# A Mamba scan whose states are turned by fp32 products with the identity instead of TensorE's transpose mode

## The chip, the cores and the metric

The kernel runs on one core of a Trainium2 chip. TensorE (PE) multiplies, VectorE (DVE), ScalarE (ACT) and GpSimd (POOL) work elementwise, and DMA queues move data. Each engine takes its instructions in the order in which the program lists them and waits on semaphores for the others. The metric is the device time of one execution in microseconds, as the median of several runs; lower is better.

## What is computed

A network of four layers on an image batch `x` of 2 x 256 x 32 x 32, all in fp32: two Mamba blocks, a convolution attention, linear attention with a mixture of experts, softmax attention with a second mixture of experts. Only the Mamba blocks matter here. With d = 512 inner channels, n = 16 states and L = 1024 tokens per image, a block computes

```python
dA = jnp.exp(delta[..., None] * A)
dBu = delta[..., None] * Bm[:, :, None, :] * xs[..., None]
def step(hst, ins):
    dA_t, dBu_t, C_t = ins
    hst = dA_t * hst + dBu_t
    y_t = jnp.einsum('bdn,bn->bd', hst, C_t)
    return (hst, y_t)
_, ys = jax.lax.scan(step, h0, (...))
y = jnp.swapaxes(ys, 0, 1) + xs * Dp
y = y * jax.nn.silu(res)
out = y @ out_w + out_b
```

Each block has input projections, a causal convolution of four taps and a softplus ahead of this, and a layer norm behind it.

## The kernel before

Both images together are 2048 tokens, taken as four chunks of 512 tokens per block, so eight chunks in all (`units`). Channels lie on the 128 partitions, four groups of them (`NDC`), tokens along the free dimension.

`Mamba.front` prepares a chunk: projections (L323), the convolution as products with diagonal matrices (L351), softplus and `du` (L396 to L431; the elementwise part of it on POOL at L425 to L431). `Mamba.scan` is the chunk's main loop over the 16 states. For each state n:

- a DMA broadcasts the row of B over the partitions (L477), and POOL makes `du * B` in two halves of 128 x 1024 (L481), into `h` tiles. Six such tiles exist, so three states' worth.
- for each of the four channel groups, ACT makes the decay `exp(delta * A)` into one of three PSUM tiles `da` (L490), and DVE runs the recurrence along the tokens in place, a scan of 512 steps (L494).
- `rest` sums over the states with the weight C. C is a number per token and h has tokens along the free dimension, so h is turned: for each 128 tokens, TensorE turns four 128 x 128 blocks into a PSUM tile `ht` of 128 tokens x 512 channels (L460; three such tiles), and DVE adds C times it to `ya` (L469). For states 0 and 10 ACT makes the product instead (L467).

`rest` is a generator: the turns of a state and their reads are issued one step at a time between the scans of the next states, through `before`. Between them `paced` also issues steps of the next chunk's `front`, of the last chunk's `back` and of the weights for the convolution behind the Mamba blocks (`taps.make`). In the eighth chunk there is no next front; 112 steps of that convolution (`early`, L818) are issued there instead.

`Mamba.back` finishes a chunk: gates (L517), then per channel group one PSUM sum of the skip term (L540) and of the two partial sums `ya` and `yb`, turned back by plain products with the identity (L545), the gating (L549), the output projection (L557, L561), the layer norm and its transposes (L192, in a helper).

The order in the source is not the order of the program: a scheduler with a cost for every instruction decides, engine by engine, what is listed ahead of what, within the dependencies and the numbers of buffers. The program carries the order that it chose.

A turn and the product that turns `ya` back are written differently. `nc.tensor.transpose(out, in, ident)` is a matmul instruction in transpose mode; L545 is `nc.tensor.matmul(out, lhsT=in, rhs=ident)`, whose result is `in` transposed times the identity.

Of the kernel before, what the change touches and what calls it, by code (L numbers as in the profile page):

```python
# [19 lines left out]
P = 128  # L20
# [226 lines left out]
class Mamba:  # L247
# [187 lines left out]
    def scan(self, j, before, between, start=False):  # L435

        net, nc, m, scanp = self.net, self.net.nc, self.m, self.scanp
        xs, bd, ct, delta, du = self.chunks[j]
        state, first = self.state, self.first(j)
        ya = self.two.tile([P, TPC, DI], F32, tag="ya", name=f"{m}_ya_{j}")
        yb = self.one.tile([P, TPC, DI], F32, tag="yb", name=f"{m}_yb_{j}")
        self.chunks[j] = xs, ya, yb
        G = 2
        half = [P, G, TC]

        def keep(n, hs):  # L450
            for g, h in enumerate(hs):
                nc.scalar.copy(state[:, n, g * G : (g + 1) * G], h[:, :, TC - 1])

        def rest(n, hs):


            for i in range(TPC):
                ps = self.ps_ht.tile([P, DI], F32, tag="ht", name=f"{m}_ht_{j}_{n}_{i}")
                for dc in range(NDC):
                    nc.tensor.transpose(  # L460
                        ps[:, dc * P : (dc + 1) * P], hs[dc // G][:, dc % G, i * P : (i + 1) * P],
                        net.ident,
                    )
                yield
                c = ct[:, i, n : n + 1]
                if n in (0, self.ASIDE):
                    nc.scalar.activation((yb if n else ya)[:, i, :], ps, AF.Copy, scale=c)  # L467
                else:
                    nc.vector.scalar_tensor_tensor(  # L469
                        ya[:, i, :], ps, c, ya[:, i, :], ALU.mult, ALU.add  # L470
                    )
                if i == 0 and first:
                    keep(n, hs)

        for n in range(NS):
            b = scanp.tile([P, TC], F32, tag="b", name=f"{m}_b_{j}_{n}", bufs=4)
            nc.sync.dma_start(b, bd[n].partition_broadcast(P))  # L477
            hs = []
            for g in range(NDC // G):
                h = scanp.tile(half, F32, tag="h", name=f"{m}_h_{j}_{n}_{g}", bufs=6)  # L480
                made = (nc.vector if start and n == 0 else nc.gpsimd).tensor_mul(  # L481
                    h, du[:, g * G : (g + 1) * G, :], b.unsqueeze(1).to_broadcast(half)
                )
                hs.append(h)
            self.product = made
            for dc in range(NDC):
                da = self.ps_da.tile([P, TC], F32, tag="da", name=f"{m}_da_{j}_{n}_{dc}")
                i = dc * NS + n
                with net.tc.issue_after(net.loaded.ins):
                    net.decayed = nc.scalar.activation(  # L490
                        da, delta[:, dc, :], AF.Exp, scale=self.aneg[:, i : i + 1]
                    )
                h = hs[dc // G][:, dc % G, :]
                nc.vector.tensor_tensor_scan(  # L494
                    h, da, h, 0.0 if first else state[:, n, dc : dc + 1], ALU.mult, ALU.add
                )


                next(before, None)
                if n or dc:  # L500
                    next(between, None)
            before = chain(before, rest(n, hs))
        for _ in between:
            pass
        return before
# [1295 lines left out]
```

## Time and profile before

| | |
|---|---|
| median of 3 runs | 2160.94 us (2155.56 to 2163.15) |
| the profiled execution | 2164.79 us as timed, span 2163.1 us |
| mean granted TensorE clock | 0.909 of full speed |
| PE, busy | 1894.6 us (88%), 9652 instructions |
| PE weight loads (PEld), busy | 1343.4 us (62%), 9652 instructions |
| DVE, busy | 1403.5 us (65%), 2173 instructions |
| ACT, busy | 891.1 us (41%), 1589 instructions |
| POOL, busy | 1027.9 us (48%), 726 instructions |

The profile is taken by the hardware in one execution. A matmul shows as two records, a load of the stationary operand (PEld) and the multiplication (PE). Matmuls overlap, and their ends are modelled, so PE's busy time is not its work. The span in 40 slices of 54 us, in tenths of busy time:

```profile
PE   6889799897988888799999999949999699859996
...
DVE  6999989999999998897414575652222534432223
...
PEclk9869888898979999799999999959999799979997
```

The Mamba blocks are the first 19 slices or so (scans run from 49.6 to 1054.1 us), and there DVE is nearly always busy. PEclk is the clock that TensorE was granted. What follows, up to the end of the span, is the rest of the network; the change doesn't touch it. Other views used below give one line of code's instructions with their durations, what each engine waited for, TensorE's instructions in order of time, and busy times in chosen stretches.

### The profile page before, as it was taken

How to read it: one execution, taken by the hardware profiler on the slowest of the kernel's cores; microseconds unless marked ns; L12 is line 12 of the kernel's file. 1: busy time of each engine (PE TensorE's matmuls, PEld its weight loads, DVE VectorE, ACT ScalarE, POOL GpSimd, SP SyncE). 2: the span in 40 equal slices, each digit the busy share in tenths (PEclk: the TensorE clock that was granted, in tenths of full speed). 3: DMA queues.
4: the chain of work that ended last, by engine and by line, in shares of the span. 5: the costliest groups of instructions: out<-in, count | busy, mean ns of one | idle time of the engine just before them, and what ended most of it. 6: DMA issues, size and time to landing. Idle time of an engine off the chain costs nothing.

```text
span 2163.1 us, 27234 instructions
## 1 busy us (share of the span) xinstructions
PE 1894.6 (88%) x9652; PEld 1343.4 (62%) x9652; DVE 1403.5 (65%) x2173; ACT 891.1 (41%) x1589; POOL 1027.9 (48%) x726
## 2 busy tenths in 40 slices
PE   6889799897988888799999999949999699859996
PEld 2465566555565545455655556639998467659994
DVE  6999989999999998897414575652222534432223
ACT  4677666676777667553213433311110222201111
POOL 3787887959688785964316410013332000023331
PEclk9869888898979999799999999959999799979997
DMA  3121121112112111310030100038998200069997
GB/s 108 45 69 40 42 66 40 54 35 63 45 47 61 40 49 31 82 43 25 10 55 1 49 15 10 20 116 301 329 329 306 83 10 10 20 216 328 333 331 285
DMA packets 90497, 223.85 MB, mean 103 GB/s; under 512 B 35467, under 2 KB 51728, under 8 KB 79732
## 3 DMA queue, kind: packets, MB, share of 16 engines
q1 hardware_dynamic: 77636, 198.29, 27.4%
q0 software_dynamic: 7728, 19.15, 3.0%
q10 hardware_dynamic: 4992, 4.59, 0.7%
q8 instruction: 80, 1.31, 0.3%
q14 instruction: 61, 0.50, 0.1%
HBM read 204.60 MB, written 19.37 MB: 104 GB/s over the span
## 4 chain that ended last, share of the span: by engine, by line
PE 27%; issue 14%; POOL 8%; DVE 8%; DMA 4%; ACT 1%; POOLq 0%; ACTq 0%; DVEq 0%; SPq 0%
PE acc L818 4%; POOL x L1578 3%; POOL l_yd L1628 3%; PE av L1332 3%; PE h L1155 3%; PE early_acc L818 2%; PE sc L1306 2%; DMA l_yd<-y,target 2%; DVE m_h L494 2%; PE w L1164 1%; DVE m_ya L469 1%; DMA x<-l_zd,source 1%; PE m_ht L460 1%; PE mm_t L192 1%; POOL m_h L481 1%
## 5 line engine op out<-in xcount | busy, mean ns | idle before, releaser
L481 POOL TENSOR_TENSOR m_h<-m_du,m_b 128x1024 f32<-128x1024 f32 x254 | 594.4, 2363 | 222.5 <-PE m_ht L460 124.0
L460 PEld LDWEIGHTS m_ht<-ident,m_h 128*128 128x128 f32 x2048 | 265.5, 155 | 300.7 <-issue 110.7
L460 PE MATMUL m_ht<-ident,m_h 128*128 128x128 f32 x2048 | 357.6, 304 | 98.1 <-DVE m_ya L469 71.9
L490 ACT ACTIVATE m_da<-m_delta,m_aneg 128x512 f32<-128x512 f32 x512 | 349.2, 691 | 210.5 <-DVE m_h L494 206.3
L1578 POOL DMA_INDIRECT x<-l_zd,source x82 | 84.6, 1032 | 576.1 <-DVE source L1523 218.6
L469 DVE SCALAR_TENSOR_TENSOR m_ya<-m_ht,m_ct,m_ya 128x512 f32<-128x512 f32 x448 | 319.3, 731 | 30.7 <-PE m_ht L460 30.4
L494 DVE TENSOR_TENSOR_SCAN m_h<-m_da,m_state,m_h 128x512 f32<-128x512 f32 x256 | 317.9, 1268 | 23.3 <-POOL m_h L481 14.5
L494 DVE TENSOR_TENSOR_SCAN m_h<-m_da,m_h 128x512 f32<-128x512 f32 x256 | 303.4, 1208 | 21.1 <-ACT m_da L490 13.5
L1608 PEld LDWEIGHTS h<-xts,we 128*128 128x128 f32 x2528 | 298.3, 194 | 6.1 <-issue 2.2
L1608 PE MATMUL h<-xts,we 128*128 128x128 f32 x2528 | 299.1, 277 | 1.6 <-issue 1.5
L1615 DVE TENSOR_TENSOR hid<-hid,h 128x512 f32<-128x512 f32 x79 | 54.3, 687 | 266.8 <-PE h L1608 266.8
L1614 ACT ACTIVATE hid<-h 128x512 f32<-128x512 f32 x79 | 47.2, 597 | 411.3 <-PE h L1608 411.3
L1622 PE MATMUL o<-we,hid 128*128 128x256 f32 x632 | 150.6, 380 | 3.9 <-DVE hid L1615 2.3
L1628 POOL DMA_INDIRECT l_yd<-y,target x79 | 79.0, 1000 | 136.4 <-DVE y L1627 131.6
L1622 PEld LDWEIGHTS o<-we,hid 128*128 128x128 f32 x632 | 113.7, 190 | 17.8 <-DVE hid L1615 3.0
L351 PE MATMUL m_conv<-m_pre,m_taps 128*128 128x512 f32 x240 | 114.3, 596 | 1.6 <-ACT m_gate L521 1.6
L818 PE MATMUL early_acc<-x,early 128*98 128x448 f32 (+24 forms) x308 | 98.6, 447 | 0.0
L818 PE MATMUL acc<-x,pair 128*98 128x416 f32 (+21 forms) x308 | 93.8, 453 | 0.0
L1627 DVE COPY y<-o 128x256 f32<-128x256 f32 x79 | 33.5, 425 | 70.0 <-PE o L1622 69.7
L323 PE MATMUL m_in<-x,m_in_sb 128*128 128x512 f32 x128 | 70.4, 665 | 9.2 <-ACT m_pre L327 5.4
L517 PE MATMUL m_g<-x,m_gate_sb 128*128 128x512 f32 x128 | 69.6, 650 | 7.3 <-ACT m_gate L521 4.7
L818 PEld LDWEIGHTS acc<-x,pair 128*98 128x98 f32 x308 | 48.0, 168 | 40.6 <-issue 35.4
(313 smaller groups left out, 2797.7 us busy)
## 6 DMA issues: line engine op xcount, KB each, us to landing
we<-in_l_experts_dram SPq DMA_DIRECT2D x82, 1536.0 KB, 9.4
m_b<-m_bd SPq DMA_DIRECT2D x128, 256.0 KB, 3.3
w<-in_l_w_dram SPq DMA_DIRECT2D x21, 256.0 KB, 4.1
l_zd<-l_z SPq DMA_DIRECT2D x7, 512.0 KB, 2.8
l_yl<-l_yd SPq DMA_DIRECT2D x10, 256.0 KB, 5.9
l_yl<-l_yd ACTq DMA_DIRECT2D x10, 256.0 KB, 6.5
early<-taps SPq DMA_DIRECT2D x7, 343.0 KB, 4.9
pair<-taps SPq DMA_DIRECT2D x7, 343.0 KB, 6.0
```

The source lines that it names most:

```text
L323: nc.tensor.matmul(ps, lhsT=self.in_sb[:, kc, mc * P : (mc + 1) * P], rhs=self.xt[:, kc, tok], start=(kc == 0), stop=(kc == NCC - 1),)
L351: nc.tensor.matmul(ps, lhsT=self.taps[:, dc * 4 + k, :], rhs=pre[:, dc, k : k + TC], start=(k == 0), stop=(k == 3),)
L460: nc.tensor.transpose(ps[:, dc * P : (dc + 1) * P], hs[dc // G][:, dc % G, i * P : (i + 1) * P], net.ident,)
L469: nc.vector.scalar_tensor_tensor(ya[:, i, :], ps, c, ya[:, i, :], ALU.mult, ALU.add)
L481: made = (nc.vector if start and n == 0 else nc.gpsimd).tensor_mul(h, du[:, g * G : (g + 1) * G, :], b.unsqueeze(1).to_broadcast(half))
L490: net.decayed = nc.scalar.activation(da, delta[:, dc, :], AF.Exp, scale=self.aneg[:, i : i + 1])
L494: nc.vector.tensor_tensor_scan(h, da, h, 0.0 if first else state[:, n, dc : dc + 1], ALU.mult, ALU.add)
L818: nc.tensor.matmul(a[:, lo - 16 * k : hi - 16 * k, co : co + n], lhsT=lhsT, rhs=self.x[:, kc, b, lo - r0 : hi - r0, ci : ci + n], start=(u ...
L1578: nc.gpsimd.indirect_dma_start(out=x, out_offset=None, in_=zd[:, :], in_offset=bass.IndirectOffsetOnAxis(ap=source[:, g : g + 1], axis=0), ...
L1608: nc.tensor.matmul(ps[:, at], lhsT=w12[:, s, kc, at], rhs=xt[:, kc * P : (kc + 1) * P], start=(kc == 0), stop=(kc == NCC - 1),)
L1622: nc.tensor.matmul(ps[:, :C], lhsT=ht[:, mc * P : (mc + 1) * P], rhs=w[:, 8 + mc, :], start=(mc == 0), stop=(mc == NHC - 1),)
L1628: nc.gpsimd.indirect_dma_start(out=yd[g], out_offset=bass.IndirectOffsetOnAxis(ap=target[:, g : g + 1], axis=0), in_=y, in_offset=None, bo ...
```

## The change

In `rest`, the four transposes of a turn become four matmuls with the same operands, without transpose mode: `lhsT` is the block of h, `rhs` the identity, and each is a sum of its own (`start` and `stop` both set).

```diff
                 for dc in range(NDC):
-                    nc.tensor.transpose(
-                        ps[:, dc * P : (dc + 1) * P], hs[dc // G][:, dc % G, i * P : (i + 1) * P],
-                        net.ident,
+                    nc.tensor.matmul(
+                        ps[:, dc * P : (dc + 1) * P],
+                        lhsT=hs[dc // G][:, dc % G, i * P : (i + 1) * P], rhs=net.ident,
+                        start=True, stop=True,
                     )
                 yield
                 c = ct[:, i, n : n + 1]
```

Nothing else in the source changes. The instructions are the same in number on every engine, apart from one table load of ACT, but the scheduler lists many of them in another order. The changed file is one line longer, so everything behind L463 moves down by one line.

## The prediction

> **What bounds the kernel now.** I read the list of costly groups first, then each line's own view, then the waits, the tables by stretch and the timelines.
>
> The edit is on L460, so the first question is what its successor costs. The kernel already has that instruction: L545 multiplies 128x128 fp32 blocks by the same identity, without transpose mode. Its lines:
>
> ```profile
> L460 PE MATMUL m_ht<-ident,m_h x2048: 270/273/478, 51.2 to 1059.3; 128*128 128x128 f32 x187
> L460 PEld LDWEIGHTS m_ht<-ident,m_h x2048: 137/141/356, 50.9 to 1059.1; 128*128 128x128 f32 x187
> ...
> L545 PE MATMUL m_y<-ident,m_ya x256: 272/275/421, 201.7 to 1068.1; 128*128 128x128 f32 x128
> L545 PEld LDWEIGHTS m_y<-ident,m_ya x256: 190/192/337, 201.3 to 1068.0; 128*128 128x128 f32 x128
> ```
>
> The durations (min/median/max in ns) look alike; the counts don't. The loops issue 8 chunks x 16 states x 4 x 4 = 2048 turns, and the trace has 2048 records: one each. L545 issues 8 x 4 x 4 = 128 products on ya, and the trace has 256 records: two each. The other fp32 products agree (L561: 8 x 4 x 4 = 128 in the code, 256 records). So one fp32 product is two loads and two passes in this trace, one turn is one of each.
>
> What a record costs is the pitch, not the duration, since records overlap. From TensorE's timeline:
>
> ```profile
> 449.92 0.60 PE L460 MATMUL m_ht<-ident,m_h 128*128 128x128 f32 x4
> 450.36 1.02 PE L540 MATMUL m_y<-m_xs,m_skip 128*128 128x512 f32 x2
> 451.22 1.05 PE L545 MATMUL m_y<-ident,m_ya 128*128 128x128 f32 x8
> ```
>
> Four turns take 450.36 - 449.92 = 0.44 us: 0.110 each (0.109 over long runs). The two 512-column records take 0.86, 0.43 each. Eight L545 records last 1.05 us of which the last is 0.275: (1.05 - 0.275)/7 = 0.111, so a product is 2 x 0.112 = 0.224 us.
>
> Now who sets the end of the Mamba stage (49.6 to 1054.1 us, eight chunks of 115 to 143 us):
>
> ```profile
> 658.20:778.80 120.60, 103.94 (x507) 66.76 (x505) 117.42 (x135) 84.61 (x129) 96.87 (x53) 0.92 0.16 40
> ...
> 910.90:1054.10 143.20, 136.06 (x606) 81.01 (x605) 117.93 (x132) 64.58 (x92) 84.08 (x41) 1.00 0.13 35
> ```
>
> Columns: stretch, length, busy time of PE, its loads, DVE, ACT, POOL, then the clock. In the sixth chunk DVE is busy 117.4 of 120.6 us; the other middle chunks are alike. In the eighth PE takes over: 136 of 143, because the early convolution (L818) runs there. But "busy PE" counts overlapping ends twice over, so I count its work by records times pitch. For the second quarter of the fourth chunk, 438.1 to 470.6 us (16 scans):
>
> ```profile
> L460 PE MATMUL m_ht<-ident,m_h 128*128 128x128 f32 x68 | 9.8, 276 | 0.9 <-DVE m_ya L469 0.9
> L351 PE MATMUL m_conv<-m_pre,m_taps 128*128 128x512 f32 x20 | 9.4, 593 | 0.0
> L370 PE MATMUL m_xd_ps<-m_xs,m_xp_sb 128*48 128x512 f32 x8 | 3.8, 602 | 0.2 <-ACT m_xs L363 0.2
> L545 PE MATMUL m_y<-ident,m_yb 128*128 128x128 f32 x24 | 3.2, 275 | 0.0
> L545 PE MATMUL m_y<-ident,m_ya 128*128 128x128 f32 x24 | 3.2, 275 | 0.0
> L540 PE MATMUL m_y<-m_xs,m_skip 128*128 128x512 f32 x6 | 3.1, 594 | 0.0
> ```
>
> With three more 512-wide records (L399, L517) that is 68 x 0.109 + 48 x 0.112 + 37 x 0.43 = 28.7 us of work in 32.5. There is little room.
>
> **The change, part by part.** *Passes.* 2048 x (0.224 - 0.109) = 236 us more of TensorE time, some 29 per chunk. Nothing else is added; DVE's reads (L469), POOL's products (L481) and the transfers stay in number.
>
> How much of the 29 is hidden? I repeat the count above (width/512 x 0.43 for other widths) for each quarter of each chunk, add 0.115 per turn, and take what exceeds the quarter's length. In the quarter shown: 28.7 + 7.8 = 36.5, so 4.0 over (4 from unrounded counts). Chunk by chunk: second 5.3, third 4.1, fourth 6.5, fifth 7.3, sixth 5.6, seventh 0: sum 28.8 us. The fourth quarters have 10 us to spare each, the first chunk 25, so neither gives anything. The cover is DVE's own work; where it is gone (front matmuls of the next chunk, the projections of the last one), a slot goes at PE's pace. Bounds: whole chunks instead of quarters have room for all of it (PE's work afterwards is 110 to 122 us against lengths of 119 to 132), so 0; stretches of 3.4 us instead of quarters give 73. The ring of three PSUM buffers and six h tiles spans about 2 to 3 states, 16 to 24 us, so I stay with the quarter: 29.
>
> *Eighth chunk.* PE's work there is 130.6 us in 143.2. With 248 turns at 0.115 (28.5) it is 159.1: at least 15.9 over if all idle time is used, 28.5 if none. The idle part lies mostly before 967 us, where the convolution is thin, so I take the middle, 22.
>
> *Loads.* The first load of a group that finds PE waiting is longer by 192 - 141 = 51 ns. It is on the path only where DVE waits for a turn, 28 times: 1.4 us. The second load runs beside the first pass (L545 keeps 0.112 with it).
>
> *Order.* The scheduler writes another order: the reads of turned states now trail the scans by 7 scans on average in the middle chunks (5.5 before, counted from the built order), and each chunk has a run of seven to nine scans without a read. An h tile is free for POOL only when its state is turned, and the turn needs a PSUM buffer that a read has freed. Between the read of state 1 and the first scan of state 4, DVE's work shrinks from 9 to 12 us to 2.2 to 3.4. In it must fit four groups' last turn and one POOL product of 2.36 us (L481). At one prompt turn of 4 x 0.224 + 0.27 = 1.2, that is 3.6 us: short by 0.2 to 1.4 in each of seven chunks, some 5 us. If the last turn comes 4 us after the read that frees its buffer, as it does at these places before (3.9 to 4.4 us in the timelines), 4 x 7 = 28 more. POOL's 16 elementwise products of the next front (1.27 us each, L425 to L431) also stand closer together, within three states: 16 x 1.27 + 2 x 4.73 + 2.36 = 32 against some 29 of DVE. That is 3 us a chunk, but where PE already stretches the quarter it overlaps. I take 12 for the order, ends 0 and 33. What waits behind a late read on DVE's queue is the next scan, and for that ACT's decays (L490, three PSUM buffers).
>
> A gain is possible too. Today DVE waits in the chunks before the eighth:
>
> ```profile
> DVE m_ya L469 <- PE m_ht L460: 19.7, 21, 2.3
> DVE m_h L494 <- ACT m_da L490: 17.4, 15, 2.6
> DVE m_h L494 <- POOL m_h L481: 12.0, 9, 3.2
> ```
>
> 49 us in all; a deeper lag could swallow some. I count none, since turns get slower.
>
> *Clock.* All pitches are at full clock; these chunks run at 0.74 to 0.92. The stretches that fell to half are thin ones:
>
> ```profile
> 111.82 2.49 PE L460 MATMUL m_ht<-ident,m_h 128*128 128x128 f32 x10
> ...
> 111.80:115.20 3.40, 3.17 (x14) 2.11 (x12) 3.40 (x4) 3.12 (x5) 2.61 (x2) 0.51 0.13 39
> 115.20:118.60 3.40, 1.65 (x10) 0.98 (x9) 3.40 (x5) 3.31 (x4) 3.15 (x2) 1.00 0.05 17
> 118.60:122.00 3.40, 2.45 (x8) 1.37 (x8) 3.40 (x5) 2.03 (x4) 3.40 (x2) 0.50 0.18 60
> ```
>
> After 10 short records in 3.4 us (115.2 to 118.6) the clock halves; the fuller stretch before it, which the timeline shows as almost nothing but turns, ended in a rise to 1.00. Eight products in 3.4 us are 16 records, half the time: I expect the clock near 1.00 and use the full-speed pitch.
>
> The Trainium skill, "TensorE: Matmul & The Clock Gate", section "Terms", says that transpose mode is four times faster for fp32: the rule against this change. The trace's two records against one make it 2.05. By four the extra would be 2048 x 0.327 = 670 us, and the eighth chunk alone would grow by about 69. The same page's Part 4 says that transposes do not lift the clock; the rise at 115.2 after turns alone disagrees.
>
> *Sum:* 22 + 29 + 12 + 1 = 64 us on the profiled execution's span of 2163.1 (2164.8 as timed), giving 2229. That execution lies 3.9 above the median of the runs, 2160.9, so I forecast 2225.
>
> **The rivals.** (A) *All on the path*: turns and their readers go in lockstep, nothing is hidden: 2161 + 236 = 2397. For it: PE waits for DVE's reads (71.9 us) and DVE for PE. Against: fourth quarters are half empty on PE. (B) *Hidden*: the new order spreads the passes evenly and the eighth chunk fills its idle time with little left over: within 6 us of 2161. Against: 15.9 over in the eighth even then. (C) *Faster*: the deeper lag ends DVE's 49 us of waits above, the eighth chunk pays its 16: 2161 - 49 + 16 = 2128. It decides if PE keeps below DVE in every stretch, so that no read finds its turn missing; the quarters of the second to sixth chunk speak against it. (D) *One pass*: a product by the identity stays one record at 0.112; then 2048 x 0.003 = 6 us of PE and only the order's 5 to 33: about 2175. All 256 products of L545 having two records is against it.
>
> **How the numbers follow.** Mine 0.80, A 0.05, B 0.05, C 0.04, D 0.06. The forecast's own ends: 16 in the eighth chunk alone, 2177; 28.5 + 73 + 33 + 1 = 135, 2296. A few us inside these ends, 2178 to 2292, leaves A, B, C and most of D outside, some 2 in 10. A measurement of this kernel tells 0.3% (6.5 us) from no change. Faster: C, 0.04. Same: B and a little of D, 0.07. Slower: the rest, 0.89.
>
> **What would show it.** 4096 records on the turn's line at a pitch of 0.112; the eighth chunk 16 to 28 us longer with PE over 95% busy; second and third quarters longer by 4 us or more; DVE's waits for turns well above 30.4 us; clock near 1.00 from 160 to 1050 us; nothing moved after the Mamba stage. I am wrong if the records stay 2048, or if a chunk's length follows DVE alone.

## The result and the profile after

| | median | runs | ratio to before |
|---|---|---|---|
| before | 2159.39 us | 2155.56 to 2163.15 (4, with one run more than in the table above) | |
| after | 2325.65 us | 2322.88 to 2328.68 (4) | 1.077 [1.0745, 1.0795] |

The change makes the kernel 166 us slower, where 64 were forecast and 2292 us was the upper end. The profiled execution after has a span of 2321.2 us, 158.1 more than before. The Mamba stage, from the first scan to the last, grew by 152.9 us (1004.4 to 1157.3), so the loss is there.

The costly groups of the page after, then the turn's own line (min/median/max in ns):

```profile
L482 POOL TENSOR_TENSOR m_h<-m_du,m_b 128x1024 f32<-128x1024 f32 x254 | 594.4, 2361 | 356.5 <-PE m_ht L460 218.9
...
L460 PE MATMUL m_ht<-ident,m_h 128*128 128x128 f32 x4096 | 554.7, 288 | 94.8 <-DVE m_ya L470 84.8
...
L470 DVE SCALAR_TENSOR_TENSOR m_ya<-m_ht,m_ct,m_ya 128x512 f32<-128x512 f32 x448 | 322.2, 735 | 97.8 <-PE m_ht L460 94.3
L495 DVE TENSOR_TENSOR_SCAN m_h<-m_da,m_state,m_h 128x512 f32<-128x512 f32 x256 | 315.0, 1267 | 75.5 <-POOL m_h L482 75.1
...
L495 DVE TENSOR_TENSOR_SCAN m_h<-m_da,m_h 128x512 f32<-128x512 f32 x256 | 300.4, 1206 | 52.2 <-POOL m_h L482 47.5
```

```profile
L460 PE MATMUL m_ht<-ident,m_h x4096: 271/275/582, 50.8 to 1218.7; 128*128 128x128 f32 x196
```

The same groups of POOL and DVE in the profile before:

```profile
L481 POOL TENSOR_TENSOR m_h<-m_du,m_b 128x1024 f32<-128x1024 f32 x254 | 594.4, 2363 | 222.5 <-PE m_ht L460 124.0
...
L469 DVE SCALAR_TENSOR_TENSOR m_ya<-m_ht,m_ct,m_ya 128x512 f32<-128x512 f32 x448 | 319.3, 731 | 30.7 <-PE m_ht L460 30.4
L494 DVE TENSOR_TENSOR_SCAN m_h<-m_da,m_state,m_h 128x512 f32<-128x512 f32 x256 | 317.9, 1268 | 23.3 <-POOL m_h L481 14.5 <-ACT m_da L490 8.8
L494 DVE TENSOR_TENSOR_SCAN m_h<-m_da,m_h 128x512 f32<-128x512 f32 x256 | 303.4, 1208 | 21.1 <-ACT m_da L490 13.5 <-POOL m_h L481 7.6
```

The records doubled, 2048 to 4096, as forecast; the median step from one record of the turn to the next is 111 to 112 ns. The busy time of DVE's groups hardly changed. What changed is its idle time. The waits of the reads for turns tripled, 30 to 94 us, as slower turns would make them. But the largest new item is another: the scans wait 123 us for POOL's products (75.1 + 47.5), where they waited 22 (14.5 + 7.6). POOL's products take no longer than before (594.4 us); POOL itself waits for turns, 219 us ahead of these products instead of 124.

The sixth and the eighth chunk, in the columns of the prediction's table (stretch, length, busy time of PE, its loads, DVE, ACT, POOL, then clock):

```profile
751.30:903.70 152.40, 132.10 (x771) 103.23 (x769) 119.33 (x135) 84.77 (x126) 98.16 (x54) 0.92 0.14 35
1044.10:1206.50 162.40, 159.68 (x835) 111.01 (x835) 118.17 (x131) 66.12 (x95) 77.49 (x37) 1.00 0.10 29
```

The eighth chunk is bound by PE, busy 159.7 of 162.4 us, and 19 us longer. In the sixth nobody is full: DVE's 119 us of work now take 152, and PE has idle time too. A chunk in which no engine is full, and which grew by 32 us, is not explained by more work on one engine.

### The profile page after: what moved, and what is told of

Its sections match the earlier page's. It is cut to its first block, busy times and chain, and to the rows that moved or that the text cites. A ratio compares the mean times of both kernels' runs of the same rounds, so it can differ in the third digit from the quotient of the medians.

```text
span 2321.2 us, 31349 instructions
## 1 busy us (share of the span) xinstructions
PE 2062.8 (89%) x11700; PEld 1580.7 (68%) x11700; DVE 1413.2 (61%) x2173; ACT 898.6 (39%) x1588; POOL 1030.1 (44%) x726
## 4 chain that ended last, share of the span: by engine, by line
PE 42%; issue 17%; DVE 16%; POOL 15%; ACT 4%; DMA 4%; POOLq 0%; DVEq 0%; ACTq 0%; SPq 0%
PE m_ht L460 9%; DVE m_h L495 8%; DVE m_ya L470 4%; POOL m_h L482 4%; PE early_acc L819 4%; PE m_conv L351 3%; PE acc L819 3%; POOL x L1579 3%; POOL l_yd L1629 3%; PE av L1333 2%; PE h L1156 2%; PE sc L1307 2%; DMA l_yd<-y,target 2%; PE m_g L518 2%; POOL m_ln L427 1%
## 5 line engine op out<-in xcount | busy, mean ns | idle before, releaser
L482 POOL TENSOR_TENSOR m_h<-m_du,m_b 128x1024 f32<-128x1024 f32 x254 | 594.4, 2361 | 356.5 <-PE m_ht L460 218.9
L460 PEld LDWEIGHTS m_ht<-ident,m_h 128*128 128x128 f32 x4096 | 523.8, 200 | 217.4 <-DVE m_ya L470 96.4
L460 PE MATMUL m_ht<-ident,m_h 128*128 128x128 f32 x4096 | 554.7, 288 | 94.8 <-DVE m_ya L470 84.8
L495 DVE TENSOR_TENSOR_SCAN m_h<-m_da,m_state,m_h 128x512 f32<-128x512 f32 x256 | 315.0, 1267 | 75.5 <-POOL m_h L482 75.1
L495 DVE TENSOR_TENSOR_SCAN m_h<-m_da,m_h 128x512 f32<-128x512 f32 x256 | 300.4, 1206 | 52.2 <-POOL m_h L482 47.5
L562 PE MATMUL m_out<-m_out_sb,m_xs 128*128 128x256 f32 x256 | 65.5, 400 | 0.0
```

The costliest lines, as they stand in the source:

```text
L460: nc.tensor.matmul(ps[:, dc * P : (dc + 1) * P], lhsT=hs[dc // G][:, dc % G, i * P : (i + 1) * P], rhs=net.ident, start=True, stop=True,)
L495: nc.vector.tensor_tensor_scan(h, da, h, 0.0 if first else state[:, n, dc : dc + 1], ALU.mult, ALU.add)
```

## The experiments

The kernel before, run again beside each group of variants, took 2159 to 2162 us each time. The table sums up the profiles. "Quarters" are the 16 states of a chunk in fours; each column is how much longer than in the profile of before those quarters are, added over the first seven chunks. The last columns are DVE's waits in the stage: scans for POOL, reads for turns. These sums are mine, from the starts of the scans and the waits that the trace gives. Two things have to be kept in mind. How far a column moves by itself shows in e3 below, whose first seven chunks are the same program as before: -2.2, 0.7, -4.0 and -0.1 us. And a column also changes when reads move from one quarter into another, so the main readings below go by waits and idle time.

| kernel | time, us | 1st | 2nd | 3rd | 4th quarters | eighth chunk | for POOL | for turns |
|---|---|---|---|---|---|---|---|---|
| before | 2159.4 | | | | | | 22.1 | 30.4 |
| after | 2325.65 | 12.8 | 16.9 | 42.9 | 60.9 | 19.3 | 122.5 | 90.3 |
| e1, turns in the new order | 2284.49 | 4.4 | 11.8 | 42.3 | 56.5 | 3.3 | 112.2 | 55.4 |
| e2, products in the old order | 2223.26 | 7.2 | 17.1 | 26.4 | -8.2 | 16.1 | 22.4 | 76.9 |
| e4, after with reads kept close | 2254.76 | 31.9 | 16.0 | -13.5 | 31.3 | 21.6 | 32.6 | 110.4 |
| e9, turns in the order of e4 | 2195.40 | 15.4 | 6.4 | -20.4 | 28.6 | 0.7 | 41.3 | 45.7 |
| e5, before with reads kept close | 2144.45 | 6.8 | -6.5 | -7.6 | -8.4 | -3.0 | 7.0 | 31.9 |
| e8, products in the order of e5 | 2227.17 | 33.2 | 18.5 | 7.7 | -17.0 | 16.3 | 8.6 | 103.5 |
| e12, e1 with half of POOL's front | 2232.24 | 4.4 | 9.7 | 45.0 | 2.7 | 3.8 | 55.0 | 56.3 |

### Order and passes apart (e1, e2)

The scheduler has a cost for every instruction, so the edit changed two things: what a turn costs on TensorE, and the order that is written for all engines. The two come apart if the program is scheduled with one form and the instruction is then replaced by the other:

```diff
     conv_attn_hybrid(tc, args, out)
+    for f in nc.m.functions:
+        for block in f.blocks:
+            for k, i in enumerate(block.instructions):
+                if isinstance(i, _mybir.InstMatmult) and "_ht_" in str(i.outs[0]):
+                    block.instructions[k] = _copy.replace(i, is_transpose=True)
```

on the changed kernel is e1 (the new order, one pass; an import and a count of the replaced instructions are left out here). The same loop on the kernel before, with `is_transpose=None`, is e2 (the old order, two passes).

> The new order of all engines, but every turn put back into transpose mode after the scheduler has run. Theory 'passes' (the added 236 us of TensorE work make the time): one record per turn again, 2150 to 2175 us. Theory 'order' (reads that trail further behind the scans starve POOL's h tiles): most of the loss stays, 2240 to 2330 us. If each has a share, the distance from 2159 is the order's share.

> The order of before, but every turn made a plain product after the scheduler has run. Theory 'passes': 2290 to 2350 us, near the changed kernel's 2326. Theory 'order': only the quarters in which TensorE has too much work and the eighth chunk pay, 2200 to 2240 us.

Measured: e1 2284.49 us (2284.16 to 2285.74), ratio 1.0576 [1.0558, 1.0593]; e2 2223.26 us (2220.44 to 2224.32), ratio 1.0287 [1.027, 1.0304].

The order alone costs 124.5 us, with the cheap turn. The passes alone cost 63.3. Together they cost 166, less than the sum of 188; waits that cover one another would do that, but no run shows which. DVE's groups in e1:

```profile
L470 DVE SCALAR_TENSOR_TENSOR m_ya<-m_ht,m_ct,m_ya 128x512 f32<-128x512 f32 x448 | 318.9, 734 | 57.2 <-PE m_ht L460 56.2
L495 DVE TENSOR_TENSOR_SCAN m_h<-m_da,m_state,m_h 128x512 f32<-128x512 f32 x256 | 315.0, 1267 | 73.9 <-POOL m_h L482 68.6 <-ACT m_da L491 5.1
L495 DVE TENSOR_TENSOR_SCAN m_h<-m_da,m_h 128x512 f32<-128x512 f32 x256 | 300.3, 1206 | 59.2 <-POOL m_h L482 43.6 <-ACT m_da L491 15.7
```

Nearly all of the waits for POOL are here, 112 of 123 us, with not one extra pass. In e2 they are as before:

```profile
L469 DVE SCALAR_TENSOR_TENSOR m_ya<-m_ht,m_ct,m_ya 128x512 f32<-128x512 f32 x448 | 326.9, 734 | 88.7 <-PE m_ht L460 80.8
L494 DVE TENSOR_TENSOR_SCAN m_h<-m_da,m_state,m_h 128x512 f32<-128x512 f32 x256 | 318.3, 1268 | 24.0 <-POOL m_h L481 18.2 <-ACT m_da L490 5.7
```

So the waits of scans for POOL come with the order alone. The waits of reads for PE come mostly with the passes (80.8 us in e2), but the order raises them too (56.2 in e1, 30.4 before).

The table tells where. The passes cost second and third quarters (43.5 us), the eighth chunk and a little in first quarters, and nothing in fourth quarters. The order costs third quarters (42.3) and fourth ones (56.5).

### What the passes cost, by parts (e3, e6)

e3 is e2's loop on the eighth chunk's products alone (`"m2_ht_3_" in str(i.outs[0])`, 256 of them). e6 is the same loop on the second and fourth token group of every state, 1024 products.

> The order of before, products in the eighth chunk's turns alone (256 of 2048). The prediction's term for that chunk was 22 us (16 to 28.5): 2175 to 2188 us. If the coupling of the engines counts there too, more than 2190.

> The order of before, with plain products for two of the four token groups of each state (1024 of 2048 turns, 118 us more of TensorE work). Theory 'room' (a quarter pays what exceeds its length): the same count with 0.0575 us per turn leaves 7 us over, 4 of them in the eighth chunk, so 2164 to 2174 us. Theory 'every pass costs the same share': half of the 63 us of all products, 2187 to 2195.

e3: 2178.55 us, ratio 1.009 [1.0073, 1.0107]: +18.6 for the eighth chunk. In its profile that chunk is 14.4 us longer and what follows the last scan 4.5. The other 44.7 of e2's 63.3 fall to the first seven. e6: 2175.43 us, ratio 1.0073 [1.0052, 1.0093]: +16.0, just above the 2164 to 2174 us of the count by room and far from an equal share: a quarter of the whole for half of the products. The first passes are mostly hidden and the later ones are not: what an engine with room to spare takes is not in proportion. The count by room had given about half of what was measured.

### Reads kept close to the scans (e4, e5, e7, e8, e9)

In the new order the reads trail: 7 scans on average against 5.5. From the start of the fourth chunk, in the order in which DVE runs them (S a scan, t a read):

```
before  StStStStStSSSSStSSStSStSttSStttttSStStS
after   StStStSSSSttSSSSSSSStStttStSttttStSStSt
e4      StStStStStSSSSStStStStStStStStStStStStS
```

e4 is the changed kernel in which a scan may not be listed ahead of the read that comes ahead of it in the source; e5 is the same rule in the kernel before:

```diff
-                    nc.vector.scalar_tensor_tensor(
+                    self.read = nc.vector.scalar_tensor_tensor(
...
+                with net.tc.issue_after((self.read or made).ins) if self.read else ExitStack():
-                nc.vector.tensor_tensor_scan(
+                    nc.vector.tensor_tensor_scan(
```

e7 adds the other direction to e5 (a read not ahead of its scan either). e8 is e5's order with products put in afterwards, e9 e4's order with turns, by the loop above.

> The changed kernel with one rule more for the scheduler: a scan is listed behind the read that stands before it in the source, so that reads trail the scans by 4.9 scans instead of 7. POOL's order stays bunched (4 to 8 elementwise products in a row). Theory 'trailing reads': nearly all of the order's loss returns, 2205 to 2245 us (products in the old order took 2223). Theory 'POOL's bunching' or TensorE's own order: 2290 us or more.

> The kernel of before (transpose mode) with the same rule: reads trail by 4.8 scans instead of 5.5. If trailing reads cost time there too, DVE's 22 us of waits for POOL and part of its 30 us for turns shrink: 2120 to 2150 us. If before was free of that, 2155 to 2180.

> Transpose mode with VectorE's scans and reads in the order of the source, both ways: a scan behind the read before it, a read behind the scan before it (reads trail by 5.0, strictly alternating). If only a long trail costs, 2138 to 2150 us as with the one-way rule (2144). If the one-way rule also won by reading early, 2150 to 2165.

> The order of the fifth experiment (turns, reads close, 2144 us), every turn made a plain product afterwards. Theory 'two shares' (passes pay by room, the order pays by POOL's tiles): the passes cost about as much as in the old order, 63 us, so 2195 to 2220 us, under the 2223 of the old order. If the one-way rule only moves waits about, 2220 or more.

> The order of the fourth experiment (products, reads close, 2255 us), every turn put back into transpose mode. What is left of the order's loss there should be POOL's bunched elementwise products, one wait of some 5 us in each of seven chunks: 2180 to 2210 us. If trailing reads were all of it, 2140 to 2165.

| | time, us | ratio to before |
|---|---|---|
| e4 | 2254.76 | 1.0434 [1.0417, 1.0452] |
| e5 | 2144.45 (2141.67 to 2145.36) | 0.9922 [0.9906, 0.9939] |
| e7 | 2160.89 | 0.9996 [0.9983, 1.001] |
| e8 | 2227.17 | 1.0314 [1.0296, 1.0331] |
| e9 | 2195.40 | 1.017 [1.0153, 1.0187] |

e4 takes back 71 us of the 166, and lies between its two forecasts (2205 to 2245, and 2290 or more). The third quarters, 42.9 us too long, are now 13.5 shorter than before. Their idle time on DVE is the better measure, since the rule also moves reads into other quarters: 8.1 us before, 47.0 after, 8.0 in e4. So the rule removes what made third quarters long. It makes the scheduler write the order of all engines anew, POOL's too, so it does not show the trail of the reads by itself. Fourth quarters are still 31.3 too long, and with one-pass turns (e9) 28.6, so that rest is order too, and not the trail.

The same rule in the kernel before wins 15 us (e5): the fastest version of this study, ahead of both kernels. Its waits for POOL fell from 22.1 to 7.0. Made strict both ways (e7) it wins nothing. And with products e5's order is worth nothing (e8 against e2: 2227 and 2223): DVE then waits 103.5 us for turns, and what POOL delivers earlier finds no use. So e8 missed the 2195 to 2220 us that two shares that simply add up would give: what the passes cost depends on the order, 63.3 us in the one of before, 41.2 in the new one (after less e1), 59.4 in that of e4 (e4 less e9), 82.7 in that of e5 (e8 less e5).

### POOL's bunch (e10, e11, e12)

POOL makes 16 elementwise products of the next chunk's front in each of the first seven chunks. Both orders have two runs of six of them (H and h are the two halves of a state's product for the scans, p is elementwise, o anything else; end of the fourth chunk). In the order of before two have been made earlier and two states' products stand between the runs; in the new order one state's does:

```
before  ...HhpHphppppppHhHhppppppoHhpp
after   ...HhppppppHhppppppHhppoppHhHho
e4      ...HhppppHhppppHhppppppoppHhHh
```

What that does, in e1's fourth chunk, first by DVE's timeline and then by POOL's (start, length, then the instructions; the idle time before them in brackets):

```profile
551.57 2.45 DVE L495 TENSOR_TENSOR_SCAN m_h<-m_da,m_state,m_h 128x512 f32<-128x512 f32 x2
556.53 4.81 DVE L495 TENSOR_TENSOR_SCAN m_h<-m_da,m_state,m_h 128x512 f32<-128x512 f32 x4 [2.52 <-POOL m_h L482]
...
568.80 4.81 DVE L495 TENSOR_TENSOR_SCAN m_h<-m_da,m_state,m_h 128x512 f32<-128x512 f32 x4 [6.58 <-POOL m_h L482]
...
582.74 1.28 DVE L495 TENSOR_TENSOR_SCAN m_h<-m_da,m_state,m_h 128x512 f32<-128x512 f32 x1 [5.01 <-POOL m_h L482]
```

```profile
524.86 4.68 POOL L482 TENSOR_TENSOR m_h<-m_du,m_b 128x1024 f32<-128x1024 f32 x2 [9.42 <-PE m_ht L460]
536.84 4.67 POOL L482 TENSOR_TENSOR m_h<-m_du,m_b 128x1024 f32<-128x1024 f32 x2 [7.31 <-PE m_ht L460]
541.80 4.70 POOL L482 TENSOR_TENSOR m_h<-m_du,m_b 128x1024 f32<-128x1024 f32 x2 [0.29 <-PE m_ht L460]
546.45 1.28 POOL L425 TENSOR_TENSOR m_du<-m_e,m_du 128x512 f32<-128x512 f32 x1
...
554.14 4.67 POOL L482 TENSOR_TENSOR m_h<-m_du,m_b 128x1024 f32<-128x1024 f32 x2
558.76 1.28 POOL L429 TENSOR_TENSOR m_delta<-m_delta,m_ln 128x512 f32<-128x512 f32 x1
...
566.42 4.64 POOL L482 TENSOR_TENSOR m_h<-m_du,m_b 128x1024 f32<-128x1024 f32 x2
575.10 1.27 POOL L425 TENSOR_TENSOR m_du<-m_e,m_du 128x512 f32<-128x512 f32 x1 [4.04 <-ACT m_du L424]
...
580.37 4.65 POOL L482 TENSOR_TENSOR m_h<-m_du,m_b 128x1024 f32<-128x1024 f32 x2
```

POOL stood idle 9.4 and 7.3 us for late turns just ahead of the bunch, and goes into it with one state's pair just made (541.80) and nothing beyond it; DVE has used that up by 554. Inside the bunch one state's pair comes every 12.3 us (566.42 - 554.14: six elementwise products and a pair), while four scans take 4.8. DVE is short by 2.5, 6.6 and 5.0 us, 14 in this chunk. Ahead of the third of these waits POOL itself waited 4.0 us for ACT (575.10).

The small lead is not what sets the new order apart. In the profile before, POOL goes into its first run of six, in the same chunk, with as much in hand, five scans' worth in both. Its timeline, then DVE's:

```profile
498.56 1.26 POOL L429 TENSOR_TENSOR m_delta<-m_delta,m_ln 128x512 f32<-128x512 f32 x1
...
506.21 9.29 POOL L481 TENSOR_TENSOR m_h<-m_du,m_b 128x1024 f32<-128x1024 f32 x4
...
508.60 1.28 DVE L494 TENSOR_TENSOR_SCAN m_h<-m_da,m_state,m_h 128x512 f32<-128x512 f32 x1 [1.22 <-POOL m_h L481]
```

There the first run costs 1.2 us, and the second, behind two states' products, 1.1. What differs is what comes between the runs, and what DVE does meanwhile: before, its scans stand between reads; in e1 it has ten scans in a row (551.57 to 573.6), and in each of the second to seventh chunks nine or ten at this place. Both programs in one view, from the start of the first run (columns as above; 546.45 to 582.74 in e1, 498.56 to 525.64 before):

```profile
546.45:582.74 36.29, 20.43 (x97) 15.40 (x96) 22.18 (x29) 17.81 (x32) 31.47 (x24) 0.74 0.10 31
498.56:525.64 27.08, 17.93 (x82) 13.98 (x83) 24.79 (x33) 15.66 (x29) 26.45 (x20) 0.67 0.09 30
```

In e1 POOL has 31.5 us of work there and DVE 22.2. By the two timelines, 74.7 of e1's 112.2 us of waits for POOL stand behind a product that POOL issued straight after elementwise ones (8.3 of 22 before), and 37.4 behind one that had itself waited.

The test is to thin the bunch. L425 and L427, a part of the computation (the correction of the rounding in softplus), are left out of the seven fronts that POOL makes:

```diff
-            eng.tensor_sub(w, e[:, dc, :], w)
+            if alone:
+                eng.tensor_sub(w, e[:, dc, :], w)
+                eng.tensor_add(ln[:, dc, :], ln[:, dc, :], w)
             yield
-            eng.tensor_add(ln[:, dc, :], ln[:, dc, :], w)
             yield
```

e10 does it in e4, e11 in the kernel before as the control, e12 in e1.

> The fourth experiment (products, reads close, 2255 us) without L425 and L427, POOL's first two of the four elementwise steps of a front (they add the rounding error of 1 + e to the softplus; this part of the computation is left out, for seven chunks). VectorE's order stays the same but for a few places. Theory 'POOL's bunching': the run of eight elementwise products shrinks to four or five, the seven waits of 32.6 us for POOL nearly vanish, 2215 to 2235 us. If TensorE's passes alone hold it there, 2245 or more.

> The kernel of before without L425 and L427 in the same way. DVE waits only 22 us for POOL there, of which 10 in the eighth chunk, that has no front: 2145 to 2160 us, so that what the last run gains beyond some 10 us is due to the bunching.

> The new order with turns of one pass (2284.5 us), and POOL's elementwise products L425 and L427 left out in the first seven fronts (a part of the computation: the correction of the rounding of 1+e in softplus); the order of DVE's scans and reads stays as it was. In the profile of the new order with turns DVE's scans wait 112 us for POOL's products; counted from the two timelines, 74.7 us of that stand behind a product that POOL issued straight after elementwise products of the next front, and 37.4 behind one that had itself waited, mostly for a turn. If the bunch of elementwise products is a cost in itself, halving it (from some 6 to 3 between two products of a state, 3.8 us less each) takes away 40 to 70 of the 74.7: 2215 to 2245 us, and the waits for POOL fall to some 45 to 75. If the bunch only stands where DVE would have waited for late turns anyway, the waits move to the turns or to ACT and no more is won than the same edit won in the order of before (10 us): 2270 to 2280.

| | time, us | against | difference |
|---|---|---|---|
| e10 | 2239.18, ratio 1.0352 [1.033, 1.0375] | e4 2254.76 | -15.6 |
| e11 | 2149.35, ratio 0.9937 [0.9916, 0.9959] | before 2162.09 | -12.7 |
| e12 | 2232.24, ratio 1.0327 [1.0308, 1.0346] | e1 2284.49 | -52.3 |

e10 missed the 2215 to 2235 that the bunch was to explain. Its waits for POOL are gone, yet its reads wait as long for turns as e4's:

```profile
L471 DVE SCALAR_TENSOR_TENSOR m_ya<-m_ht,m_ct,m_ya 128x512 f32<-128x512 f32 x448 | 328.5, 737 | 113.0 <-PE m_ht L461 107.7 <-ACT m_da L492 4.4
```

Its fourth quarters went from 31.3 to 14.8 us too long, so the place is right, but with two-pass products and close reads the turns hold the rest. As a test of the bunch by itself it was badly placed, on a kernel in which the bunch was half spread already and another engine was late. Hence e12, in the order where the bunch stands and turns are cheap. There the same edit wins 52.3 us, 40 more than in the control, and nearly all of it where the bunch is: fourth quarters fall from 56.5 to 2.7 too long, third quarters stay (42.3 and 45.0). The order of DVE's scans and reads is e1's up to single places, its ten scans in a row among them. Its scans, then POOL's and DVE's timelines at the same place:

```profile
L496 DVE TENSOR_TENSOR_SCAN m_h<-m_da,m_state,m_h 128x512 f32<-128x512 f32 x256 | 315.2, 1268 | 36.5 <-POOL m_h L483 30.9 <-ACT m_da L492 5.1
...
L496 DVE TENSOR_TENSOR_SCAN m_h<-m_da,m_h 128x512 f32<-128x512 f32 x256 | 300.4, 1207 | 40.0 <-POOL m_h L483 24.2 <-ACT m_da L492 15.4 <-ACT m_state L453 0.3
```

```profile
527.90 4.95 POOL L430 TENSOR_TENSOR m_delta<-m_delta,m_ln 128x512 f32<-128x512 f32 x4
532.81 2.51 POOL L432 TENSOR_TENSOR m_du<-m_delta,m_xs 128x512 f32<-128x512 f32 x2
535.26 4.66 POOL L483 TENSOR_TENSOR m_h<-m_du,m_b 128x1024 f32<-128x1024 f32 x2
539.87 1.27 POOL L432 TENSOR_TENSOR m_du<-m_delta,m_xs 128x512 f32<-128x512 f32 x1
541.11 4.66 POOL L483 TENSOR_TENSOR m_h<-m_du,m_b 128x1024 f32<-128x1024 f32 x2
```

```profile
537.65 4.81 DVE L496 TENSOR_TENSOR_SCAN m_h<-m_da,m_state,m_h 128x512 f32<-128x512 f32 x4 [2.17 <-POOL m_h L483]
...
543.49 4.81 DVE L496 TENSOR_TENSOR_SCAN m_h<-m_da,m_state,m_h 128x512 f32<-128x512 f32 x4 [0.16 <-POOL m_h L483]
```

The first run still has six products here, with the same lead, and still costs 2.2 us. It is the second run that shrank, from six to one, and the waits of 6.6 and 5.0 us went with it. (Behind the second of these e1 also has POOL's wait of 4.0 us for ACT at L425, a line that e12 leaves out, so not all of the 5.0 is the bunch's.) Waits for POOL fell from 112 to 55 us; of those behind elementwise products 17 are left, and those behind products that had waited are unchanged, 38.0.

So the order's cost lies in two places. In third quarters DVE's idle time grew by 38 us in e1 (8.1 to 46.3): 24.6 us of waits for POOL (none before), 15.2 of them behind products that had waited themselves and 9.3 at the first scan of state 12, behind the bunch, and 15.7 more of waits for turns. The rule for the reads takes this idle time away. In fourth quarters it grew by 50 (19.3 to 68.9), and 65.4 of it are waits for POOL (8.3 before): runs of elementwise products with one state's pair between them meet nine or ten scans in a row. Neither of the two is all of it. e9 has at most five scans in a row there and runs of four, four and six to eight products, and its scans still wait 41.3 us for POOL; e12 keeps the scans and loses the second run, and 10.9 us of idle time are left in fourth quarters.

## Why the prediction was wrong, step by step

*Two records per product, 0.112 us each.* Right: 4096 records at 111 to 112 ns. The rival of one pass is out. The clock came out at 0.91 to 1.00 in the chunks, where they had 0.74 to 1.00 before; "near 1.00" was somewhat too high.

*Eighth chunk, 22 us (15.9 to 28.5).* Right in kind and nearly in size: 18.6 (e3 as a whole; inside the chunk its profile has 14.4, e2's 16.1, that of after 19.3, with PE busy 98% of it).

*Quarters of the first seven chunks, 29, and loads, 1.* The right mechanism, sized too small: 44.7 (e2 less e3). The place was right too, mostly second and third quarters, and fourth ones gave nothing. With the eighth chunk the passes were forecast at 52 and cost 63. The room in a quarter was counted as if all of it could be used; e6 shows how it runs out.

*Order, 12 us, ends 0 and 33.* This is the step that failed. It costs 124.5 us alone (e1), and 102 on top of the products (after less e2). Three things in its working went wrong.

First, the bunch was seen and priced at "3 us a chunk", by setting 32 us of POOL's work against 29 of DVE's over three states. POOL's side came out: 31.5 us. DVE's did not. Its 29 us take in the reads, but the prediction saw one run of scans without reads per chunk, and the new order has a second, nine or ten scans long, just where the bunch is. DVE has 22.2 us of work there, POOL also waits 4.0 for ACT, which was not in the sum, and the stretch takes 36.3: DVE stands still for 14 us in this chunk, where 3 were forecast. Thinning the bunch brought 40 us over the control.

Second, the trail was priced at one place per chunk, from the read of state 1 to the scan of state 4, at 5 us in all and 33 at the upper end. That place came out about right: in e1 DVE waits 1.0 to 1.5 us for POOL ahead of that scan in six of the seven chunks, 8.6 in all. The same thing recurs at states 9 and 10, which the prediction did not price: 15.2 us of waits for POOL, with 15.7 more for turns in the same quarters.

Third, the upper end was not a bound. It took one delay of 4 us in each chunk at the place that had been examined, though the order had changed at every state.

*A gain from the deeper lag.* None in the time. Waits for ACT's decays did fall (22.2 to 4.7 us), but not with the new order alone (20.8 in e1) nor with the passes alone (19.4 in e2). All passes on the path (2397) is out too, since e2 pays 63 of 236.

*Nothing moved after the Mamba stage.* The time after the last scan is 1109.0 us before and 1114.7 after, in one profile each. The experiments lie at 1108 to 1113.5, so these few us are not claimed for anything.

What stays open: how far the two parts of the order would add up without the other's help, and how the fourth quarters' loss divides between the bunch and the scans in a row. Thinning took half of POOL's elementwise products, not all, and no run changes DVE's order while it leaves the bunch in place as it stands after.

## What to carry to other kernels

Where a scheduler writes the program, a changed instruction is two changes; price the new order by itself, at every place where the queues differ, and not just at the one that stands out. Set a run of other work on a producer against what the consumer has to do in that stretch of the new order, and not against its average over the states: here POOL's 32 us were right, and DVE's 29 were 22. Holding a consumer to its place in the order is worth a try even without the change: here it made the kernel before 0.8% faster in the one-way form, and nothing in the strict one.

## What the runs showed of the hardware

An fp32 product of a 128 x 128 block with the identity costs 2 x 0.112 us of TensorE time, the transpose mode 0.109: a factor of 2.05, by the median steps of 112 ns over 4096 records and 109 over 2048. The loads of the two-pass form are longer (median 192 ns, 141 before), and still the pitch of a record stays at 0.11 us. Half of the products cost a quarter of the time of all (16.0 and 63.3 us).
